# A graph-attention kernel on one core: 36 instead of 32 rows a group fetched outside GpSimd, used two groups later, and node numbers loaded earlier

## The chip, the core and the metric

The kernel runs on one core of a Trainium2 chip. The metric is the device time of one execution in microseconds (us): 2087.24 us is the median of three executions of the kernel before (2087.07 to 2089.44). One further execution was taken with the hardware profiler; its trace is where all durations below come from.

## The reference

There are N = 12500 nodes of 128 features and 212500 edges, sorted by their destination node. The layer is one block of graph attention with 8 heads of 16 features:

```
Q, K, V = x @ WQ, x @ WK, x @ WV              # N x 128 each
Eh      = edge_attr @ WE                       # one row an edge
score   = exp(clip(sum over 16 of K[src] * Q[dst] / 4 * Eh, -5, 5))    # edge x head
wV, Z   = segment sums over dst of V[src] * score and of score
h       = x + wV / (Z + 1e-6)
h       = batch norm of h over the nodes, times gamma, plus beta
out     = layer norm of (x + h) over the features
```

The irregular part is `K[src]` and `V[src]`: for each edge, one row of 256 numbers (1 KB) is fetched from a table in memory, at an address known only from the data.

## The kernel before

**Table stage.** The first 88 us project all nodes to a table `kvd` (N rows of K and V, 1 KB each) in DRAM. The inputs of the first eight groups are projected directly, so that these groups need no gather from the table.

**Groups.** The edges stand in tiles of 128 (one edge a partition). A group `g` is 8 tiles (two windows of 4), and there are 208 groups; the last has 5 tiles. One group passes through a software pipeline written out by hand: the loop `for g in range(NG - 2)` at line 820 issues, in a fixed order, pieces of groups `g - 3` to `g + 5`. Every engine runs its own instructions in that order and waits on semaphores.

- SyncE (SP) issues the loads: `load(g + 4)` for the edge features `ea` (L518, three buffers), `load_rel(g + 5)` for the relative node numbers `rb` (L429, two buffers; only for groups 0 to 15 and 204 to 207, other groups get them four at a time by `load_quad`, L415), and its share of the row fetches (below).
- GpSimd (POOL) gathers the table rows: one indirect DMA a tile (`gather`, L227), eight a group, into one of nine slots. A slot comes free when VectorE has done `message(g)` (L647), its last reader.
- VectorE (DVE) does `products(g)` (L622, which needs the gathered rows), `both_halves(g + 1)` (L601), `scores` (L629), `message(g)` (L647), the one-hot matrices (L549 to L563) and the small steps on sums.
- TensorE (PE) does the projections of edge features and queries, the turning back and the segment sums (`gather_sum`, L663).
- ScalarE (ACT) does the exponentials (`clip_exp`, L638 and L639), the copies from PSUM, the windows of the nodes (`q_window`, L538) and its share of the row fetches.

**Rows without GpSimd.** For some groups, the eighth tile isn't gathered by GpSimd. Its 128 rows are fetched by 128 plain DMAs of 1 KB each, whose addresses are read from `row_ids` into registers: one TENSOR_LOAD reads the addresses of a share (L277), then each row is one DMA (L284). `fetch_rows(g, engine, a, b)` does this in groups 8 on: 32 rows a group, the first 20 on SP's queue at the top of the iteration, the other 12 on ScalarE's queue after `q_mid(g + 3)`. Four groups fill one tile `byrow` (three buffers), and it is used three groups (`ROW_LAG`) after the group that fetched its last row: groups 14, 18, 22 and so on, 49 in all (`row_plan`). In such a group `products` works on 4, 3 and 1 tiles: the last piece waits on VectorE's queue (`rows_there`, L291) for the semaphore that counts the rows' landing.

**Node numbers.** `q_window(g)` reads two node numbers into ScalarE's registers (TENSOR_LOAD, L533) and copies two windows of 64 columns from `hx` (L538).

From group 199 on, each slot that comes free is filled by `load_x` with four blocks of x for the last stage (L505, SP's queue, after `message(g)`).

**The end.** The last two groups are written out after the loop (L874 to L935). There `share(g - 2)` (`denom`, `recip`, `attn`) stands ahead of `products(g, (0,))`; `attn` (L679) has one buffer, whose reader is `add_x` (L688) on TensorE. Then come the norms and the output, 40 us.

Of the kernel before, what the change touches and what calls it, by code (L numbers as in the profile page):

```python
# [8 lines left out]
F32 = mybir.dt.float32  # L9
BF16 = mybir.dt.bfloat16  # L10
# [7 lines left out]
P = 128  # L18
# [4 lines left out]
U = 4  # L23
# [5 lines left out]
RUN = 64  # L29
ROWS = P  # L30
FIRST_ROW = 8
ROW_LAG = 3
SP_ROWS = 20
ACT_ROWS = 12
RQ = 4
NSEM = 6

# [22 lines left out]
def row_plan(sizes):  # L60


    full = sizes.count(U) // 2
    groups, end = [], P
    while FIRST_ROW + -(-end // (SP_ROWS + ACT_ROWS)) - 1 + ROW_LAG < full:
        groups.append(FIRST_ROW + -(-end // (SP_ROWS + ACT_ROWS)) - 1 + ROW_LAG)
        end += P
    return groups
# [7 lines left out]
def gnn_kernel(  # L76
# [37 lines left out]
    wp = lps.enter_context(tc.tile_pool(name="work", bufs=2))  # L114
    tps = ExitStack()
    tab = tps.enter_context(tc.tile_pool(name="table", bufs=1))
    late = []
# [115 lines left out]
    def issue(n=0):  # L233
        while len(queued) > n:
            f, *a = queued.pop(0)
            f(*a)
# [10 lines left out]
    by_row, fill = {}, {}  # L247
    row_loads = []
    n = SP_ROWS + ACT_ROWS
    row_tiles = row_plan(usizes)  # L250
# [15 lines left out]
    def parts(g, a, b):  # L266
        return [(a, b - 1), (b - 1, b)] if g in by_row and b == G else [(a, b)]

    def fetch_rows(g, et, a, b):
        if g not in fill:  # L270
            return
        p, c, at = fill[g]
        b = min(b, tot - at)
        if b <= a:
            return
        eng = {ET.SP: nc.sync, ET.Activation: nc.scalar}[et]
        _, offs = nc.values_load_multi_w_load_instructions(  # L277
            row_ids[p:p + 1, c + a:c + b], engines=(et,), min_val=0, max_val=(N - 1) * 8 * P,
            skip_runtime_bounds_check_because="node ids")
        for r, off in enumerate(offs, at + a):  # L280
            k = row_tiles[r // P]
            if r % P == 0:
                by_row[k] = late[0].tile([P, 1, 2 * P], F32, name="byrow", bufs=3)
            d = eng.dma_start(by_row[k][r % P:r % P + 1, 0, :].bitcast(U8), kvb[ds(off, 8 * P)].unsqueeze(0))  # L284
            d.then_inc(rows_in[r // P % NSEM], 16)
            tc.no_tile_sem_insts.add(d.ins.name)
            tc.add_to_no_dep_group(f"rows{k}", d.ins)

    def rows_there(g):
        k = row_tiles.index(g)  # L290
        w = nc.vector.wait_ge(rows_in[k % NSEM], 16 * P * (k // NSEM + 1))  # L291
        tc.declare_fence(w.ins, group=f"rows{g}")

    def own(g, a, b, step):
        if g in by_row and b == G and b - a == 1:
            tc.declare_no_dep(step.ins, group=f"rows{g}", reason="the semaphore of the rows")
# [57 lines left out]
    def within(f, g):  # L354
        return f(g) if 0 <= g < NG else None
# [54 lines left out]
    RB = {}  # L410

    def load_quad(q):
        t = late[0].tile([P, RQ, U * P], BF16, name="rbq", bufs=2)
        for h in (0, 1):
            nc.sync.dma_start(t[h * WN:(h + 1) * WN].rearrange("p k d -> p (k d)"), bass.AP(  # L415
                tensor=relT[h].tensor, offset=relT[h].offset + at_half[2 * RQ * q + h] * P,
                ap=[[0, WN], [1, RQ * U * P]]))
        for k in range(RQ):
            RB[RQ * q + k] = t[:, k, :]
# [3 lines left out]
    def load_rel(g):  # L423
        if g // RQ in quads:
            return
        RB[g] = wp.tile([P, U * P], BF16, name="rb", bufs=2)
        for h in (0, 1):
            n = usizes[2 * g + h]
            nc.sync.dma_start(RB[g][h * WN:(h + 1) * WN, :n * P], bass.AP(  # L429
                tensor=relT[h].tensor, offset=relT[h].offset + at_half[2 * g + h] * P, ap=[[0, WN], [1, n * P]]))  # L430
# [76 lines left out]
    EA, OH, OT, Q3, XW, BASE, MSG, QE, OS, AT, AGG, WT, PW = ({} for _ in range(13))  # L507
# [4 lines left out]
    def halves(g):  # L512
        return [(0, usizes[2 * g]), (usizes[2 * g], nt(g))]
# [15 lines left out]
            project(g, a, lambda: turned().rearrange("p (a b) d -> p a (b d)", b=2), True)  # L529
            yield  # L530

    def q_window(g):
        _, BASE[g] = nc.values_load_multi_w_load_instructions(  # L533
            base_i[0:1, 2 * g:2 * g + 2], engines=(ET.Activation,), min_val=0, max_val=N,
            skip_runtime_bounds_check_because="node ids")
        XW[g] = wp.tile([P, P], F32, name="xw", bufs=8)
        for h in (0, 1):
            nc.scalar.activation(XW[g][:, h * WN:(h + 1) * WN], hx[:, ds(BASE[g][h], WN)], AF.Copy)  # L538
# [59 lines left out]
    def both(g, h):  # L598
        a, b = halves(g)[h]
        t = WT[g][h][:, :(b - a) * P]  # L600
        nc.vector.tensor_tensor(t, t, QE[g][h], op=OP.mult)  # L601
# [12 lines left out]
    def products(g, hs=(0, 1)):  # L614
        if 0 in hs:
            PR[g] = wp.tile([P, G, P], F32, name="p", bufs=1)
        for i in hs:
            a, b = halves(g)[i]
            for c, d in parts(g, a, b):
                if d - c == 1 and g in by_row:  # L620
                    rows_there(g)
                step = nc.vector.tensor_tensor(PR[g][:, c:d, :], KV[g](c, d, 0), PW[g][i][:, c - a:d - a, :], op=OP.mult)  # L622
                own(g, c, d, step)
# [46 lines left out]
    def denom(g):  # L670
        RZ[g] = wp.tile([P, H], F32, name="rz", bufs=2)
        nc.vector.tensor_scalar(RZ[g], OS[g][:, P:], 1e-6, None, op0=OP.add)

    def recip(g):
        nc.vector.reciprocal(RZ[g], RZ[g])

    def attn(g):
        AT[g] = wp.tile([P, P], F32, name="at", bufs=1)
        nc.vector.scalar_tensor_tensor(  # L679
            AT[g].rearrange("p (h d) -> p h d", d=DH), OS[g][:, :P].rearrange("p (h d) -> p h d", d=DH),  # L680
            keep[:, g:g + 1], RZ[g][:, :, None].to_broadcast([P, H, DH]), op0=OP.mult, op1=OP.mult)
# [46 lines left out]
    def both_halves(g):  # L728
        both(g, 0)
        both(g, 1)  # L730
# [9 lines left out]
    for q in range(NQ):  # L740
# [13 lines left out]
        k = q - first_step  # L754
# [56 lines left out]
    def within_checks(g):  # L811
        if g >= first_check and (g - first_check) % every == 0:
            check((g - first_check) // every)

    def share(g):
        denom(g)
        recip(g)
        attn(g)

    for g in range(NG - 2):  # L820
        within(load, g + 4)
        within(load_rel, g + 5)
        if (g + 6) % RQ == 0 and (g + 6) // RQ in quads:
            load_quad((g + 6) // RQ)
        fetch_rows(g, ET.SP, 0, SP_ROWS)
        within(products, g)
        within(both_halves, g + 1)
        step = within(add_x, g - 3)
        step = within(q_mm, g + 3) or step
        if step is not None and queued and g >= FIRST_ROW + 4:  # L830
            pace(step)
        issue()
        within(gather_sum, g - 1)
        if g + 1 < nxg and g + 1 not in SLOT:
            for _ in project_main(g + 1):
                pass
        within(turn_back, g + 1)
        within(scores, g)
        within(clip_exp, g)
        within(q_hi, g + 3)  # L840
        within(x_out, g - 3)
        within(sums_out, g - 1)
        within(q_lo, g + 2)
        within(denom, g - 2)
        within(recip, g - 2)
        within(attn, g - 2)
        within(q_window, g + 4)
        within(turned_onehot, g + 3)
        within(ehqe, g + 2)
        within(q_mid, g + 3)  # L850
        fetch_rows(g, ET.Activation, SP_ROWS, SP_ROWS + ACT_ROWS)
        within(message, g)
        within(onehot, g + 1)
        if g == 2:
            load_last()
        for r in runs[1:]:
            if g == max(4, r[0] // 2 - 12):
                place(r)
        within_checks(g)
        while free and todo and not pending:  # L860
            load_x()
        bn_parts(2 * g - 5, 2 * g - 3)
        if g == NG - 5:
            assert done >= set(range(NPRE))
            norm_first()
        if g == 4:
            nc.vector.tensor_scalar(row_ids, row_ids, 8 * P, None, op0=OP.mult)
        if g == FIRST_ROW - 1:
            tps.close()
            late.append(tps.enter_context(tc.tile_pool(name="late", bufs=1)))  # L870
        if g == FIRST_ROW - 2:
            free.append(NSLOT)
            load_kv()
    last = NG - 1  # L874
    g = last - 1
# [2 lines left out]
    within_checks(last)  # L878
    flag = [nc.values_load(bad_i[0:1, 0:1], min_val=0, max_val=1 << 20,
                           skip_runtime_bounds_check_because="a count")]  # L880
    share(g - 2)
    gather_sum(g - 1)
    sums_out(g - 1)
    products(g, (0,))
    both_halves(last)
    step = add_x(g - 3)
    if queued:
        pace(step)
# [313 lines left out]
```

## Time and profile before

| what | value |
|---|---|
| median of three executions | 2087.24 us (2087.07 to 2089.44) |
| the profiled execution, whole time | 2092.52 us |
| its span in the trace | 2090.7 us |
| busy: PE, DVE, POOL, ACT | 80%, 79%, 75%, 30% of the span |
| indirect DMAs from the table `kvd` | 1548, first at 88.1 us, last at 2034.4 us |
| row DMAs: SP and ACT | 3920 and 2352 (49 tiles of 128) |
| mean granted TensorE clock | 0.935 |

The profiled execution took 5.3 us more than the median; 1.8 us of it lie outside the span. In the trace's answers a line such as `DVE p L622 <- DVEq L291: 71.3, 18, 5.2` says that VectorE, ahead of line 622, waited 71.3 us in total, 18 times, at most 5.2 us, for what its own queue did at line 291. In a timeline the columns are start and length in us, engine, line, operation, output<-inputs, and in brackets the idle time ahead of it and what ended it. "SPq" and "ACTq" are instructions that a queue processor executes, DMA issues among them.

### The profile page before, as it was taken

The page shows a single profiled execution, that of the slowest core. Times are in us where ns is not written, and L with a number is a line of the kernel's source. Part 1 is how long each engine was busy: PE and PEld are TensorE (multiplying, and loading weights), DVE is VectorE, ACT ScalarE, POOL GpSimd, SP SyncE. Part 2 cuts the span into 40 slices and gives each one's busy share as a digit, 9 for nine tenths or more (in the row PEclk, how much of TensorE's full clock was granted, in tenths as well). Part 3 has the DMA queues.
Part 4 walks back from the last instruction along what each step waited for, and adds up shares of the span by engine and source line. Part 5 has one row for each costly group of instructions (what it writes and reads, how often), then busy time and mean ns, then how long its engine had stood idle before and what let it go on. Part 6 is the DMA issues. An engine that isn't in the chain of part 4 may idle for free. (4 is left out here: it accounts for less than half of the span.)

```text
span 2090.7 us, 44264 instructions
## 1 busy us (share of the span) xinstructions
PE 1676.2 (80%) x9414; PEld 1095.7 (52%) x9414; DVE 1643.1 (79%) x3679; ACT 631.2 (30%) x2480; POOL 1561.5 (75%) x1648
## 2 busy tenths in 40 slices
PE   7898888878878888878777877777787778787877
PEld 6565554555555555555455555454454445554557
DVE  4568898888888887888787877878877778887887
ACT  2343233332233332322222222322222222222226
POOL 7677777777777777777777777777777777777775
PEclk9999999999999999999999899999999999999999
DMA  8865666666666666666666666666666665665674
GB/s 288 288 190 165 181 187 183 180 181 179 189 181 188 180 180 180 188 182 182 185 172 188 171 181 177 171 180 177 172 182 176 180 179 170 180 178 171 184 238 125
DMA packets 165317, 387.29 MB, mean 185 GB/s; under 512 B 41861, under 2 KB 76846, under 8 KB 165038
## 3 DMA queue, kind: packets, MB, share of 16 engines
q0 software_dynamic: 76352, 207.20, 35.0%
q1 hardware_dynamic: 79620, 171.95, 28.1%
q10 hardware_dynamic: 9066, 5.22, 1.0%
q14 instruction: 202, 1.65, 0.3%
q8 instruction: 77, 1.26, 0.2%
HBM read 364.59 MB, written 19.63 MB: 184 GB/s over the span
## 5 line engine op out<-in xcount | busy, mean ns | idle before, releaser
L227 POOL DMA_INDIRECT slot<-kvd,srcs x1548 | 1472.3, 951 | 479.3 <-issue 410.6
L663 PE MATMUL ps_a<-msg,oh 128*128 128x136 f32 (+1 forms) x3322 | 547.6, 306 | 0.9 <-DVE msg L647 0.9
L663 PEld LDWEIGHTS ps_a<-msg,oh 128*128 128x128 f32 (+1 forms) x3322 | 443.3, 176 | 83.7 <-issue 59.2
L588 PE MATMUL ps_e<-ea,w_e 128*128 128x512 f32 x832 | 432.9, 646 | 23.2 <-DMA ea<-eaT 20.6
L622 DVE TENSOR_TENSOR p<-slot,ps_t 128x512 f32<-128x512 f32 (+1 forms) x410 | 263.7, 663 | 210.9 <-DMA slot<-kvd,srcs 192.0
L638 ACT ACTIVATE ps_m<-s 128x64 f32<-128x64 f32 (+1 forms) x209 | 47.5, 227 | 1200.5 <-DVE s L637 845.0
L609 PE MATMUL ps_t<-ident,wt 128*128 128x128 f32 x1661 | 247.3, 291 | 102.7 <-DVE wt L601 100.7
L688 PE MATMUL ps_m<-ident,at 128*128 128x128 f32 x412 | 98.1, 321 | 234.4 <-DVE oh L552 230.5
L601 DVE TENSOR_TENSOR wt<-wt,ps_q 128x512 f32<-128x512 f32 x416 | 265.2, 678 | 3.1 <-PE ps_q L596 3.1
L609 PEld LDWEIGHTS ps_t<-ident,wt 128*128 128x128 f32 x1661 | 195.9, 147 | 130.7 <-DVE wt L601 123.9
L629 DVE TENSOR_REDUCE s<-p 128x64 f32<-128x1024 f32 (+1 forms) x209 | 251.5, 1203 | 0.1
L590 ACT ACTIVATE wt<-ps_e 128x512 f32<-128x512 f32 x416 | 229.1, 585 | 44.2 <-PE ps_e L588 43.0
L647 DVE TENSOR_TENSOR msg<-slot,ps_m 128x1024 f32<-128x1024 f32 (+2 forms) x209 | 241.2, 1155 | 1.2 <-ACT ps_m L638 1.1
L688 PEld LDWEIGHTS ps_m<-ident,at 128*128 128x128 f32 x412 | 63.6, 194 | 325.3 <-ACT q L578 308.3
L588 PEld LDWEIGHTS ps_e<-ea,w_e 128*128 128x128 f32 x832 | 156.4, 209 | 142.8 <-issue 93.6
L596 PE MATMUL ps_q<-ot,q 64*128 64x512 bf16 x1248 | 173.1, 384 | 0.0
L596 PEld LDWEIGHTS <-q 64*128 64x128 bf16 x1248 | 44.5, 95 | 194.9 <-issue 170.1
L549 DVE TENSOR_TENSOR oh<-ps_m,rel_i 128x512 f32<-128x512 f32 x208 | 141.6, 681 | 0.0
L538 ACT ACTIVATE xw<-hx 128x64 f32 x416 | 84.0, 248 | 102.2 <-issue 86.6
L679 DVE SCALAR_TENSOR_TENSOR at<-os,keep,rz 128x128 f32<-128x128 f32 x208 | 73.1, 352 | 25.8 <-PE ps_m L688 1.5
L693 ACT ACTIVATE hx<-ps_m 128x64 f32 x412 | 90.7, 220 | 8.1 <-PE ps_m L689 1.2
L569 PE MATMUL ps_m<-w_q,xw 128*128 128x128 f32 x416 | 85.7, 290 | 3.2 <-DVE oh L552 2.7
(174 smaller groups left out, 1568.6 us busy)
## 6 DMA issues: line engine op xcount, KB each, us to landing
ea<-eaT SPq DMA_DIRECT2D x207, 512.0 KB
byrow<-kvd SPq DMA_DIRECT2D x3920, 1.0 KB
byrow<-kvd ACTq DMA_DIRECT2D x2352, 1.0 KB
slot<-kvd,srcs POOLq DMA_INDIRECT x1548
rbq<-relT SPq DMA_DIRECT2D x94, 256.0 KB
kvd<-slot SPq DMA_DIRECT2D x12, 512.0 KB
kvd<-t SPq DMA_DIRECT2D x12, 512.0 KB
slot<-xT SPq DMA_DIRECT2D x24, 256.0 KB
```

What stands on the lines that cost most here:

```text
L227: return nc.gpsimd.indirect_dma_start(out=out, out_offset=None, in_=table, in_offset=bass.IndirectOffsetOnAxis(ap=srcs[:, e:e + 1], axis=0))
L549: nc.vector.tensor_tensor(one, iota_ps[:, None, :].to_broadcast([P, n, P]), r[:, :n, None].to_broadcast([P, n, P]), op=OP.is_equal)
L588: nc.tensor.matmul(eh, w_e, EA[g][:, a:b, :].rearrange("p a b -> p (a b)"), start=True, stop=True)
L590: nc.scalar.activation(t[:, :(b - a) * P], eh, AF.Copy)
L596: nc.tensor.matmul(QE[g][h], Q3[g][r, k, :], OT[g][r, :(b - a) * P], start=(k == 0), stop=(k == 2))
L601: nc.vector.tensor_tensor(t, t, QE[g][h], op=OP.mult)
L609: nc.tensor.transpose(ps[:, j, :], WT[g][h][:, j * P:(j + 1) * P], ident)
L622: step = nc.vector.tensor_tensor(PR[g][:, c:d, :], KV[g](c, d, 0), PW[g][i][:, c - a:d - a, :], op=OP.mult)
L629: nc.vector.tensor_reduce(SS[g][:, a:b, :], PR[g][:, a:b, :].rearrange("p t (h d) -> p t h d", d=DH), axis=AX.X, op=OP.add)
L647: step = nc.vector.tensor_tensor(MSG[g][:, a:b, :P].rearrange("p t (h d) -> p t h d", d=DH), KV[g](a, b, P).rearrange("p t (h d) -> p t h ...
L663: nc.tensor.matmul(AGG[g][WN if j >= n else 0:], OH[g][j], MSG[g][:, j, :], start=(j == 0), stop=(j == n - 1))
L688: nc.tensor.matmul(ps, AT[g], ident, start=True, stop=False)
```

## The change

- `SP_ROWS` 20 to 21 and `ACT_ROWS` 12 to 15: 36 rows a group, so that a tile is filled in 3.6 groups.
- `ROW_LAG` 3 to 2 and `byrow` with two buffers: a tile is used two groups after its last fetch. With both, the groups that use one are 13, 17, 20, 24, 27, 31 and so on to 205: 55 tiles. The last fetch, in group 203, holds 20 rows, all of them SP's.
- `rb` has three buffers.
- The reading of the node numbers becomes `q_base`, which the loop calls for group `g + 4` ahead of `scores` and `clip_exp`; on ScalarE's queue the TENSOR_LOAD then stands after the row fetches of the iteration before and ahead of the exponentials.
- At the end, `attn(g - 2)` comes after `products(g, (0,))` and `both_halves(last)`; `gather_sum(g - 1)` and `sums_out(g - 1)` are written after it. TensorE's order stays as it was.

```
-ROW_LAG = 3
-SP_ROWS = 20
-ACT_ROWS = 12
+ROW_LAG = 2
+SP_ROWS = 21
+ACT_ROWS = 15
...
-                by_row[k] = late[0].tile([P, 1, 2 * P], F32, name="byrow", bufs=3)
+                by_row[k] = late[0].tile([P, 1, 2 * P], F32, name="byrow", bufs=2)
...
-        RB[g] = wp.tile([P, U * P], BF16, name="rb", bufs=2)
+        RB[g] = wp.tile([P, U * P], BF16, name="rb", bufs=3)
...
-    def q_window(g):
+    def q_base(g):
         _, BASE[g] = nc.values_load_multi_w_load_instructions(
             base_i[0:1, 2 * g:2 * g + 2], engines=(ET.Activation,), min_val=0, max_val=N,
             skip_runtime_bounds_check_because="node ids")
+
+    def q_window(g):
+        if g not in BASE:
+            q_base(g)
...
         within(turn_back, g + 1)
+        within(q_base, g + 4)
         within(scores, g)
...
-    share(g - 2)
-    gather_sum(g - 1)
-    sums_out(g - 1)
+    denom(g - 2)
+    recip(g - 2)
     products(g, (0,))
     both_halves(last)
+    attn(g - 2)
+    gather_sum(g - 1)
+    sums_out(g - 1)
     step = add_x(g - 3)
```

More of the change, by code (lines that the diff above doesn't have):

```diff
@@ L880, in gnn_kernel @@
                            skip_runtime_bounds_check_because="a count")]
-    share(g - 2)
+    denom(g - 2)
+    recip(g - 2)
+    products(g, (0,))
+    both_halves(last)
+    attn(g - 2)
     gather_sum(g - 1)
     sums_out(g - 1)
-    products(g, (0,))
-    both_halves(last)
     step = add_x(g - 3)
```

## The prediction

> **What bounds the kernel now.** I read the page's groups first, then the waits of each engine, then the timeline of SP and VectorE, then the end. GpSimd comes first:
>
> ```profile
> L227 POOL DMA_INDIRECT slot<-kvd,srcs x1548 | 1472.3, 951 | 479.3 <-issue 410.6
> ```
>
> ```profile
> POOL slot L227 <- issue: 426.5, 1397, 0.3
> ...
> POOL slot L227 <- DVE msg L647: 3.7, 4, 2.8
> ```
>
> One gather is 0.95 us, and 0.30 us of issue stand ahead of nearly every one; GpSimd has waited for a free slot for 3.7 us only. The first starts at 88.1, the last at 2034.4: 1946.3 us for 1547 steps, 1.258 us each, with no hole. So the length between table and end is the number of gathers times 1.258. With 32 rows a group from elsewhere a group costs GpSimd (8 - 32/128) x 1.258 = 9.75 us.
>
> VectorE runs freely at 7.5 us a group (first products at 188.53, 196.04, 203.56) and waits for two things, one after the other in the run. From 200 to 880 us:
>
> ```profile
> DVE p L622 <- DVEq L291: 71.3, 18, 5.2
> ...
> DVE p L622 <- DMA slot<-kvd,srcs: 4.1, 5, 1.8
> ```
>
> and from 900 to 2030 us:
>
> ```profile
> DVE p L622 <- DMA slot<-kvd,srcs: 183.2, 89, 5.1
> ```
>
> Up to 880 us the row tile is late, later the gathers are. The late row is SP's, which issues without a pause:
>
> ```profile
> 361.58 0.37 SPq L518 DMA_DIRECT2D ea<-eaT  x1
> 363.53 6.38 SPq L284 DMA_DIRECT2D byrow<-kvd  x20
> 370.01 0.37 SPq L518 DMA_DIRECT2D ea<-eaT  x1
> 371.96 6.43 SPq L284 DMA_DIRECT2D byrow<-kvd  x20
> 378.49 0.37 SPq L518 DMA_DIRECT2D ea<-eaT  x1
> 378.91 1.10 SPq L415 DMA_DIRECT2D rbq<-relT  x2
> ```
>
> The hole of 1.5 us ahead of each train of rows is the TENSOR_LOAD of its addresses (1.44). Group 10's first row starts at 202.83, group 106's at 1062.27: 8.95 us a group, hardly a wait in it. VectorE uses a row 5 to 8 us after SP's last issue (group 30: last issue over at 361.47, use at 366.82). SP is thus slower than VectorE, faster than GpSimd, and it started late:
>
> ```profile
> 170.73 1.08 SPq L429 DMA_DIRECT2D rb<-relT  x2
> 171.85 0.58 SPq L518 DMA_DIRECT2D ea<-eaT  x1
> 178.32 1.08 SPq L429 DMA_DIRECT2D rb<-relT  x2
> 181.24 6.45 SPq L284 DMA_DIRECT2D byrow<-kvd  x20
> ```
>
> From 172.5 to 178.3 SP waited with `rb` of group 13 for the buffer that `turned_onehot(11)` (L559) was still reading.
>
> **The change part by part.**
>
> *Gathers.* 55 row tiles instead of 49: 1542 gathers, 6 x 1.258 = 7.5 us less on the chain that sets the end. This is the gain.
>
> *SP, 21 rows.* One more row: a step is 0.332 us (mean from row to row between 200 and 1050 us). One more address: the TENSOR_LOAD takes 0.48 for 2 addresses, 0.77 for 12, 1.37 for 20 (shortest of each); between the first two 0.03 an address, between the last two 0.075. I take 0.03 and keep 0 and 0.075. That makes 8.95 + 0.36 = 9.31 us a group (9.28 to 9.36). GpSimd will need (8 - 36/128) x 1.258 = 9.71. SP stays the faster, by 0.4 us.
>
> *Lag 2, and `rb` with three buffers.* A row is wanted one group sooner, some 8 us, while SP is already late. Against it SP starts sooner: `rb` of group 13 then waits for `turned_onehot(10)` (over at 170.7), and what ends last is the `ea` load, which needs the projection of group 9 (over at 171.6). So ea at 171.7, rb at 172.3, addresses at 173.5 instead of 179.5: 6 us. VectorE's position is set back by 8 - 6 - (rounding of the tile's end) in the first groups. Is GpSimd then blocked on slots? Group g needs the slot of group g - 9. Groups 17 and 18 have it at once or 2.6 us early, as now; group 22 starts its gathers at 228.9 and `message(13)` ended at 218.3. The wait for the first tile, at group 13, will be about 6 us, so some 3 us of margin remain after the one gather less. GpSimd isn't blocked: 0, at worst 3 us (start not advanced).
>
> *Two `byrow` buffers.* The first row of tile k + 2 is issued at least three groups after the last of tile k, 2 x 9.31 us and more of SP's time; tile k is used some 6 us after its last row and read a last time 6 us later. 12 against 18: no wait.
>
> *ScalarE.* Three more rows, 0.345 each by its mean step: 1.0 us. From the exponential at 1015.96 to the last row issued at 1022.75 are 6.8 us; with the rows, the address read ahead (0.67) and its gap, less the 0.43 that `xw` waited for it, 8.1 us a group. That is more than VectorE's 7.5, less than SP's 9.31; it takes slack, 0 on the end. The last row's landing, 6.3 + 4.7 + 4 us after a group's second products, comes before the use two groups on at 15.8; barely, and it would be swallowed by the wait for SP or GpSimd. In groups 3 to 7, where ScalarE's evacuations come right ahead of the exponentials, the read delays them by at most 0.1 each: 0.4 us, bounds 0 and 2. The added load of `row_ids` and the wider memset: 0.3, bounds 0 and 0.5.
>
> *VectorE.* A group with a row tile takes 0.2 us longer; 6 more, 1.2 us spread over the run, hidden under its waits. If the cover were gone: 1.2.
>
> *The end.* Here VectorE waits at
>
> ```profile
> 2032.78 0.35 DVE L679 SCALAR_TENSOR_TENSOR at<-os,keep,rz 128x128 f32<-128x128 f32 x1 [1.47 <-PE ps_m L688]
> 2033.05 0.68 DVE L622 TENSOR_TENSOR p<-slot,ps_t 128x512 f32<-128x512 f32 x1
> 2033.64 0.88 DVE L601 TENSOR_TENSOR wt<-wt,ps_q 128x384 f32<-128x384 f32 x2
> 2034.44 0.55 DVE L622 TENSOR_TENSOR p<-slot,ps_t 128x384 f32<-128x384 f32 x1
> ```
>
> with the products of group 206 behind it. Moved, products and both halves run from 2031.3, `attn` at 2032.8, the second products at 2033.05: 1.4 us less. VectorE's last stretch without a hole begins with the second products of group 205 at 2024.07. That group becomes a row group, so its last gather ends 7.5 + 1.26 us sooner and its row would be wanted at 2024.07 + 0.55 - 8.8 = 2015.8. SP's chain says when it's there. Group 8's first row at 181.2 - 6 = 175.2, group 10 at 21.6 later, group 199 after 189 x 8.95 = 1692 and 191 x 0.36 = 69: 1957.4. From there to group 203 it was 50.15 (four blocks of x each time, L505), 1.6 of it a wait for `rb`'s buffer that goes: 48.6 + 4 x 0.36 = 50.0, so 2007.4. Its 20th row is issued 6.2 later, 2013.6, and lands 3.4 (as at the end now) to 8 us on: 4.5, 2018.1. So VectorE waits 2.3 us there; its next operation starts at 2018.3 instead of 2024.67: -6.4, with `attn` -7.8. It can't come sooner than the last gather: 2035.3 - 7.5 + 3.8 = 2031.6 for the last products, now at 2041.03, -9.4.
>
> *Sum.* -7.8 + 0.4 + 0.3 = -7.1, -7 taken: 2085.5 against the profiled 2092.5, and 2080.2 against the median of 2087.24, since the 5.3 us between them are not the change's.
>
> **The rivals.**
>
> *SP is a little dearer and becomes the bound (slower).* It has to issue 196 groups in a row; each 0.01 us a group is 2 us at the end. Up to 0.35 there is no wait at group 205 at all and -9 stands; at 0.36, -7; at 0.39 the gain is gone; at 0.42, through fetches of code or a dearer address, it is +4.7. For it: SP is at work all the time, and the blocks of x at the end hit it. Against it: the row step of 0.332 hardly varies. 0.16, of which 0.05 fall within 0.2%.
>
> *SP is cheaper.* -9, the bound set by the last gather. 0.13.
>
> *The start isn't advanced* (another wait holds SP's first row, such as the row tiles' place, which the table's buffers must leave; their last reader ends at 172.1, against). Then the whole of SP's chain is 6 us later, and GpSimd stops 3 us at group 22: -1 to +3. 0.08.
>
> *The transfers bound it, whoever issues them.* The DMA engines are 62 to 66% busy all along (by stretches of 330 to 560 us), and the gathers' chain is made of 0.95 + 0.30 us on GpSimd, not of landings; the bytes are the same. Then: 0, less the 1.4 of the end. 0.04. The Trainium skill has this as a rule against the change: on the page "DMA: Bandwidth & Descriptors", section "Issuing engines are not separate DMA queues", all queues run on the same 16 engines, and issuing from several saves only the time to initiate a DMA, usually small. By that rule the sum would be about -1; here the time to initiate is 1.258 us of GpSimd's chain for each tile, so the trace doesn't bear it out.
>
> **How the numbers follow.** Forecast 0.59, all faster; cheaper SP 0.13, faster; dearer SP 0.16 (0.05 same, 0.11 slower); late start 0.08 (0.06 same, 0.02 slower); transfers 0.04 (same). Changes within 0.2%, 4.2 us, are what a measurement of this kernel can hardly tell from none. Faster 0.72, same 0.15, slower 0.13. The range leaves out about 2 in 10: from -10.2 (the bound at -9 and 1.2 of the runs' spread) to +0.8 over the two cases near none, 2077 to 2088.
>
> **What would show it.** Right: 1542 gathers back to back at 1.258, the last near 2027; SP's first row near 175; 9.3 us from train to train; VectorE's waits at L291 grown to 150 to 250 us in some 40 of 55 tiles and those for gathers shrunk below 100, with the length set by neither. `attn` without a wait. Wrong: a hole of GpSimd at groups 17 to 30; a train step of 9.4 or more; a wait of over 5 us at L291 in group 205.

## The result, and the profile after

The changed kernel takes 2392.41 us (median of four, 2390.69 to 2394.97) against 2087.59 us for the kernel before (2087.07 to 2089.44): a ratio of 1.146, 95% interval 1.144 to 1.148. The forecast was 2080.2. The time went up by 305 us.

In the runs called disturbed below, the kernel before took 3092 to 3164 us (medians) as well, and in the traces SP's trains of 20 or 21 rows took 11.0 to 12.5 us (medians) instead of 6.4 to 6.8, from a cause that isn't known; from those runs only the lengths of single address loads are used.

The page of the changed kernel names the engine at once. These are its chain of work that ended last (by engine, then by line) and three of its groups. Lines from L538 on stand four to seven lower than before: L642 is the exponential, L697 `x_out`, L581 `qr` of `q_mid`, L563 `turned_onehot`, L533 now the reading in `q_base`.

```profile
ACTq 40%; issue 27%; ACT 16%; PE 10%; DVE 5%; DMA 2%; POOL 0%; DVEq 0%; SPq 0%
ACTq L284 30%; ACTq L533 6%; ACT wt L594 4%; ACTq L277 3%; PE ps_a L667 3%; ACT xw L542 3%; ACT hx L697 2%; ACT ps_m L642 2%; ACT q L582 1%; DVE msg L651 1%; ACT os L672 1%; PE ps_e L592 1%; PE ps_t L348 1%; ACT q L577 1%; PE ps_t L613 1%
...
L227 POOL DMA_INDIRECT slot<-kvd,srcs x1542 | 1459.7, 947 | 728.0 <-issue 385.2
...
L581 DVE SCALAR_TENSOR_TENSOR qr<-ps_m,q 128x128 f32<-128x128 f32 x208 | 60.6, 291 | 616.3 <-ACT hx L697 611.7
L642 ACT ACTIVATE ps_m<-s 128x64 f32<-128x64 f32 (+1 forms) x209 | 47.5, 227 | 1664.6 <-PE ps_e L592 670.8
```

ScalarE's queue and ScalarE hold 56% of the chain, the row fetches (L284) alone 30%, though ScalarE computes for only 600 us. The exponential's idle 1664.6 us is the time in which its own queue reads addresses and issues rows. The releasers printed ahead of it are mostly matmuls that don't feed it. In the lap below the one printed ends at 1042.12, while VectorE's scores have been ready since 1039.17 and the queue's read of the node numbers ends last, at 1042.68. The waits of all engines, then SP's, show who stands behind it:

```profile
DVE qr L581 <- ACT hx L697: 611.7, 199, 5.1
PE ps_m L692 <- DVE oh L556: 542.9, 192, 5.2
...
POOL slot L227 <- PE ps_m L573: 295.0, 177, 4.3
```

```profile
SPq L518 <- PE ps_e L592: 335.8, 133, 11.2
```

In 199 groups VectorE waits 3 us, by the profile for the copies to `hx`; `message`, the one-hot matrices and the products stand behind that wait. TensorE waits for the one-hots, GpSimd's first gather of a group for the `q_mm` that paces it, and SP's `ea` load, with the rows behind it, for the projection that frees its buffer. There is no wait at L291 in the whole run. One lap of ScalarE, in its timeline (start and length in us; ACTq is its queue):

```profile
1031.85 0.23 ACT L642 ACTIVATE ps_m<-s 128x64 f32<-128x64 f32 x1 [8.59 <-PE ps_q L600]
1032.01 0.24 ACT L643 ACTIVATE msg<-s 128x64 f32<-128x64 f32 x1
1032.15 0.26 ACT L577 ACTIVATE q<-ps_m 128x128 bf16<-128x128 f32 x1
1032.31 0.47 ACT L697 ACTIVATE hx<-ps_m 128x64 f32 x2
1032.68 0.28 ACT L672 ACTIVATE os<-ps_a 128x136 f32<-128x136 f32 x1
1032.84 0.40 ACT L542 ACTIVATE xw<-hx 128x64 f32 x2
1033.13 1.08 ACT L594 ACTIVATE wt<-ps_e 128x512 f32<-128x512 f32 x2
1034.09 0.33 ACT L582 ACTIVATE q<-qr 128x128 bf16<-128x128 f32 x1
1036.73 5.15 ACTq L284 DMA_DIRECT2D byrow<-kvd  x15
1042.83 0.23 ACT L642 ACTIVATE ps_m<-s 128x64 f32<-128x64 f32 x1 [8.41 <-PE ps_t L613]
```

and the same place before:

```profile
1018.76 0.31 ACT L578 ACTIVATE q<-qr 128x128 bf16<-128x128 f32 x1
1018.82 3.93 ACTq L284 DMA_DIRECT2D byrow<-kvd  x12
1024.30 0.23 ACT L638 ACTIVATE ps_m<-s 128x64 f32<-128x64 f32 x1 [5.23 <-DVE s L637]
```

Before, the first row follows `q_mid` at once, and after the last row ScalarE waits 1.5 us for VectorE's scores. After, there are 2.3 us between `q_mid` and the first row, and the lap closes on itself: 10.98 us from exponential to exponential, with no wait for another engine in it. So the granted TensorE clock, 0.871 after and 0.935 before, isn't what makes the lap long. The 2.3 us are not shown as work; they are the end of the TENSOR_LOAD of the row addresses (L277), which the view of the tile `row_ids` gives as shortest/median/longest in ns. Before:

```profile
L277 SPq TENSOR_LOAD <-row_ids x196: 1372/1442/1764, 179.5 to 2014.0; - x196
L277 ACTq TENSOR_LOAD <-row_ids x196: 768/810/992, 179.5 to 2009.5; - x196
```

and after:

```profile
L277 SPq TENSOR_LOAD <-row_ids x196: 1383/1662/1954, 171.9 to 2313.1; - x196
L277 ACTq TENSOR_LOAD <-row_ids x195: 3226/3377/3571, 178.0 to 2304.8; - x195
```

Three more addresses, 15 for 12, and ScalarE's load takes 3.38 us instead of 0.81. It starts while ScalarE still computes, so 2.3 of it stand in the lap. GpSimd's gathers, unbroken before, have a hole in nearly every group:

```profile
1034.35 0.95 POOL L227 DMA_INDIRECT slot<-kvd,srcs  x1 [0.30 <-issue]
1037.46 0.94 POOL L227 DMA_INDIRECT slot<-kvd,srcs  x1 [2.17 <-PE ps_m L573]
1038.71 0.95 POOL L227 DMA_INDIRECT slot<-kvd,srcs  x1 [0.30 <-issue]
```

The last gather starts at 2269.9 us, not at 2027, and the exponential of group 207 comes 75 us behind it.

### The profile page after: what moved, and what is told of

It reads as the page before. It is cut to its first block, busy times and chain, and to the rows that moved or that the text cites. A ratio compares the mean times of both kernels' runs of the same rounds, so it can differ in the third digit from the quotient of the medians.

```text
span 2393.2 us, 45857 instructions
## 1 busy us (share of the span) xinstructions
PE 1773.3 (74%) x9414; PEld 1228.0 (51%) x9414; DVE 1653.0 (69%) x3691; ACT 600.2 (25%) x2480; POOL 1548.5 (65%) x1642
## 4 chain that ended last, share of the span: by engine, by line
ACTq 40%; issue 27%; ACT 16%; PE 10%; DVE 5%; DMA 2%; POOL 0%; DVEq 0%; SPq 0%
ACTq L284 30%; ACTq L533 6%; ACT wt L594 4%; ACTq L277 3%; PE ps_a L667 3%; ACT xw L542 3%; ACT hx L697 2%; ACT ps_m L642 2%; ACT q L582 1%; DVE msg L651 1%; ACT os L672 1%; PE ps_e L592 1%; PE ps_t L348 1%; ACT q L577 1%; PE ps_t L613 1%
## 5 line engine op out<-in xcount | busy, mean ns | idle before, releaser
L667 PE MATMUL ps_a<-msg,oh 128*128 128x136 f32 (+1 forms) x3322 | 669.9, 354 | 0.8 <-DVE msg L651 0.8
L667 PEld LDWEIGHTS ps_a<-msg,oh 128*128 128x128 f32 (+1 forms) x3322 | 557.7, 215 | 99.9 <-issue 87.8
L692 PE MATMUL ps_m<-ident,at 128*128 128x128 f32 x412 | 121.0, 385 | 552.6 <-DVE oh L556 542.9
L581 DVE SCALAR_TENSOR_TENSOR qr<-ps_m,q 128x128 f32<-128x128 f32 x208 | 60.6, 291 | 616.3 <-ACT hx L697 611.7
L642 ACT ACTIVATE ps_m<-s 128x64 f32<-128x64 f32 (+1 forms) x209 | 47.5, 227 | 1664.6 <-PE ps_e L592 670.8
L592 PE MATMUL ps_e<-ea,w_e 128*128 128x512 f32 x832 | 391.1, 592 | 0.7 <-ACT wt L594 0.7
L651 DVE TENSOR_TENSOR msg<-slot,ps_m 128x1024 f32<-128x1024 f32 (+3 forms) x209 | 240.7, 1153 | 0.4 <-ACT ps_m L642 0.3
L613 PE MATMUL ps_t<-ident,wt 128*128 128x128 f32 x1661 | 217.3, 273 | 2.1 <-ACT t L325 0.6
L573 PE MATMUL ps_m<-w_q,xw 128*128 128x128 f32 x416 | 109.4, 357 | 3.1 <-DVE oh L556 2.7
L693 PE MATMUL ps_m<-xw,ident 128*128 128x128 f32 x412 | 105.9, 350 | 0.0
L573 PEld LDWEIGHTS ps_m<-w_q,xw 128*128 128x128 f32 x416 | 90.2, 267 | 5.1 <-issue 2.5
```

Of the source, the lines that this page charges most:

```text
L592: nc.tensor.matmul(eh, w_e, EA[g][:, a:b, :].rearrange("p a b -> p (a b)"), start=True, stop=True)
L613: nc.tensor.transpose(ps[:, j, :], WT[g][h][:, j * P:(j + 1) * P], ident)
L651: step = nc.vector.tensor_tensor(MSG[g][:, a:b, :P].rearrange("p t (h d) -> p t h d", d=DH), KV[g](a, b, P).rearrange("p t (h d) -> p t h ...
L667: nc.tensor.matmul(AGG[g][WN if j >= n else 0:], OH[g][j], MSG[g][:, j, :], start=(j == 0), stop=(j == n - 1))
L692: nc.tensor.matmul(ps, AT[g], ident, start=True, stop=False)
```

## The experiments

The theories. **A (the start):** the load is dear because the addresses now start at column 21 of their row of `row_ids`, no multiple of four. **B (the number):** more than 12 addresses, or an odd number, are dear. **C (the place):** the node numbers read ahead make ScalarE's loads dear. Later **D**: something else of the change costs too, **E**: ScalarE's lap counts in full, **F**: the shorter lag.

### What makes the load dear

The kernel before with other shapes of read, the same rows being fetched:

```
+        k = g % 8
...
-            row_ids[p:p + 1, c + a:c + b], ...
+            row_ids[p:p + 1, c + a - (k if a else 0):c + b + (0 if a else k)], ...
...
+        offs = offs[k:] if a else offs[:b]
```

> The kernel before, with reads of other shapes and the same rows fetched: in group g, with k = g mod 8, ScalarE reads its addresses from column 20 - k on (12 + k addresses, the last 12 used), and SP reads 20 + k from column 0 (the first 20 used). Theory A (the start): ScalarE's loads are cheap from columns 20 and 16 (0.8 and 1.0 us) and dear from 13, 14, 15, 17, 18 and 19: 0.22 for each address, 2.9 to 4.2 us. SP's grow by 0.22 for each address past a multiple of four. Theory B (the number): all with more than 12 are dear, the 16 from column 16 too. Theory C (the place): none is dear, under 1.3 us all. The time of the whole: by A a group on ScalarE is 6.8 + 2 on the mean = 8.8 to 9.3, under GpSimd's 9.75, so 2087 to 2150 us.

Measured, median of about 25 loads of each shape:

| ScalarE: first column | 20 | 19 | 18 | 17 | 16 | 15 | 14 | 13 |
|---|---|---|---|---|---|---|---|---|
| addresses | 12 | 13 | 14 | 15 | 16 | 17 | 18 | 19 |
| us | 0.82 | 2.94 | 3.14 | 3.37 | 1.07 | 3.82 | 4.03 | 4.25 |

From columns 20 and 16 the load is cheap, from the six others it costs 0.22 us for each address (a straight line through the six points has that slope and 0.07 us at nought). 16 addresses from column 16 are cheaper than 13 from 19. All eight of ScalarE's reads end at column 32, so the number of addresses is a multiple of four exactly where the start is: the table alone doesn't tell the two apart. SP's reads do. They all start at column 0, and with odd numbers took 1.67 us (21), 2.06 (23), 1.90 (25) and 2.30 (27), where 0.22 an address would be 4.6 to 5.9. So a number that is no multiple of four is not dear from such a start; what is left beyond a multiple of four costs some 0.2 each, over 1.44 for 20 in the kernel before. (SP's loads of even numbers scatter in this disturbed run, those of 24 between 0.11 and 1.76, and are left out.) A holds, B falls; on ScalarE itself no such number was read from such a start. The kernels that followed agree. The changed kernel with one column more read:

```
-            row_ids[p:p + 1, c + a:c + b], ...
+            row_ids[p:p + 1, c + a // 4 * 4:c + b], ...
...
+        offs = offs[a % 4:]
```

> The changed kernel, but ScalarE's read of its row addresses (L277) starts one column earlier, at column 20 instead of 21 of its row of row_ids, and the first of the 16 addresses is dropped. Theory A (the start): the load took 3.4 us instead of 0.8 because it starts at a column that is no multiple of four, so that each of the 15 addresses costs 0.22 us by itself. From column 20 it takes 0.9 to 1.1 us, a group on ScalarE falls from 10.98 to 8.6 us, GpSimd's gathers run back to back again, and the time is what the prediction gave, 2075 to 2090 us. Theory B (the number): more than 12 addresses, or an odd number, are dear on ScalarE: the load of 16 takes 3.4 us or more and the time stays at 2390 or above. Theory C (the place): the node numbers read ahead of the exponentials make ScalarE's loads dear, whatever the start: 3.4 us, 2390.

the changed kernel without `within(q_base, g + 4)`:

> The changed kernel without the node numbers read ahead: they are read in q_window, as in the kernel before. Theory A (the start) and theory B (the number): the load of 15 addresses still takes 3.4 us. 0.78 and a gap of 0.15 leave the line ahead of the exponentials, about 0.45 come back ahead of the copies of the windows: 10.5 us a group instead of 10.98, 195 x 0.48 = 94 us less, about 2300 us (2280 to 2320). Theory C (the place): the load takes 0.9 us again, and the time is 2075 to 2090.

and with `SP_ROWS` 20 and `ACT_ROWS` 16:

> The changed kernel with the 36 rows a group shared as 20 by SP and 16 by ScalarE, whose addresses then start at column 20. Theory A (the start): the load takes 0.9 to 1.1 us, a group on ScalarE 8.6 + 0.35 = 8.9 to 9.0 us, one on SP 8.95; both under GpSimd's 9.71: 2072 to 2090 us. Theory B (the number): 3.5 us and more, a group over 11.2 us, above 2430 us. Theory C (the place): the load stays at 3.4 us, above 2390 us.

ScalarE's load took 1.05, 3.37 and 1.05 us: C falls too. All four runs were disturbed, so their times tell nothing; undisturbed ones follow further down, but not for the second kernel.

The Trainium skill says on its page "Runtime: NRT & Kernel Launch", section "Instruction fetch mechanics", that a TENSOR_LOAD costs about 200 ns a register, in bulk as well; it says so of the registers that the runtime loads, while the row here is a tile of the kernel. The six dear shapes agree with that (0.22 us); 12 addresses in 0.82 and 16 in 1.07 us do not, and here the measurement decides.

### What the load costs the kernel

The first of these kernels again, undisturbed:

> The changed kernel with ScalarE's addresses read from column 20 (16 of them, the first dropped), for a time that is not disturbed: in the two runs so far every engine's queue stopped for some 10 us in most groups, in the kernel before just as here. Theory A (the load of 15 addresses from column 21 is the whole loss): 8.7 us a group on ScalarE, gathers at 1.258, 2075 to 2090 us against 2087 for the kernel before. Theory D (something else of the change costs too): above 2110 us.

2133.68 us (2131.04 to 2136.76), ratio 1.022 (1.020 to 1.024). The one column takes away 259 of the 305 us, but the kernel is still slower than before, so D holds: A explains 85% of the loss and not all of it. Tile `row_ids` and the waits of this run (lines one lower again):

```profile
L277 SPq TENSOR_LOAD <-row_ids x196: 1392/1688/2021, 172.1 to 2056.0; - x196
L277 ACTq TENSOR_LOAD <-row_ids x195: 1010/1057/1234, 178.2 to 2038.1; - x195
```

```profile
DVE qr L582 <- ACT hx L698: 247.6, 173, 5.1
...
DVE p L627 <- DVEq L292: 93.3, 23, 11.1
```

The gathers are nearly unbroken again: 1.261 us each on the mean, the last at 2029.8. But VectorE is far behind them: its last products start at 2080.3, 50 us after the last gather, where before they started 7 us after. VectorE waits for ScalarE's copies in 173 groups. SP too has become slower than forecast: 9.59 us a group from group 8 to 104, 8.99 before. It waits no more than before: from its last row to the next address load are 0.85 us on the mean, 0.84 before. Its last address load starts at 2056.0, 42 us later than the 2014.0 of before, and VectorE's last long wait of the run is for the rows that follow it, in group 205 (SP's queue, then VectorE):

```profile
2057.54 6.44 SPq L285 DMA_DIRECT2D byrow<-kvd  x20
```

```profile
2058.27 1.14 DVE L627 TENSOR_TENSOR p<-slot,ps_t 128x512 f32<-128x512 f32 x2
2065.33 0.29 DVE L627 TENSOR_TENSOR p<-byrow,ps_t 128x128 f32<-128x128 f32 x1 [5.91 <-DVEq L292]
```

This is the third sign that the prediction named for a wrong forecast. With the load repaired, SP's chain ends the run.

### Where the other 46 us are

20 and 16 rows, which gives both queues cheap loads:

```
-SP_ROWS = 21
-ACT_ROWS = 15
+SP_ROWS = 20
+ACT_ROWS = 16
```

> The changed kernel with 20 rows by SP and 16 by ScalarE (addresses from columns 0 and 20), for an undisturbed time. The run with 21 and 15 and a cheap read on ScalarE left SP at 9.59 us a group where the prediction had 9.31: its load of 21 addresses took 1.69 us, that of 20 takes 1.44. Theory A, for both queues (an address beyond a multiple of four costs 0.2 us on either): SP is back at 8.95 to 9.0 us a group, ScalarE at 8.5 + 0.35 = 8.9, GpSimd's 9.71 sets the length again, and the gain of the prediction comes: 2077 to 2082 us against 2087.6. Theory E (ScalarE's longer group, which VectorE waits for in each group, costs by itself): 2088 us or more.

2142.84 us (2138.96 to 2153.31), ratio 1.025 (1.023 to 1.027). The gain that A promised for two cheap loads doesn't come: SP's load is back at 1.43 us and the time has not dropped. But the row that SP gave up went to ScalarE, so this doesn't say that SP was not what held the run before. VectorE's waits and SP's:

```profile
DVE qr L581 <- ACT hx L697: 342.2, 187, 5.1
```

```profile
SPq L518 <- PE ps_e L592: 215.9, 87, 11.2
```

SP has time to wait (1.54 us from last row to next load); here ScalarE's lap holds it. The same without the node numbers read ahead:

```
-        within(q_base, g + 4)
```

> 20 rows by SP, 16 by ScalarE, both loads cheap, and the node numbers read in q_window as in the kernel before. With the read ahead this gave 2142.8 us (ratio 1.0249): SP's load of 21 addresses, theory A's second half, was not what held it, ScalarE's group took 9.73 us on the mean (8.7 where it waits for nothing, and 1.0 of waits for TensorE and VectorE on the mean), every group of it in VectorE's way. Theory E (ScalarE's group counts in full): taking the read from the head of the exponentials takes 0.95 us from the line and gives 0.57 back ahead of the windows, so 9.35 us a group and 2143 - 190 x 0.38 = 2071, bounded below by the gathers at 2078: 2076 to 2095 us. If the read ahead has no part in it (the rows themselves hold VectorE up): 2130 us or more.

2117.00 us (2108.85 to 2123.54), ratio 1.014 (1.012 to 1.017). The read ahead costs about one hundredth of the time, some 22 us of 2087, with these shares; both E's 2076 to 2095 and the 2130 or more of the other case are missed. The rows alone, in the kernel before:

```
-ACT_ROWS = 12
+ACT_ROWS = 16
```

> The kernel before with one part of the change: 36 rows a group, 20 by SP and 16 by ScalarE (both loads cheap), still used three groups later from three buffers, rb with two, the node numbers and the end as before. With the lag of two, three rb buffers and the new end the same share gave 2117.0 us (ratio 1.0144), VectorE waiting 186 us for ScalarE's copies to hx, 93 us for rows and 31 us for gathers. Theory E (ScalarE's group of 8.8 us, waits for TensorE in it, is too long whatever the lag): VectorE's wait for hx stays near 186 us and the time near 2117 us (2105 to 2125). Theory F (the shorter lag: rows are waited for, the wait delays ScalarE's next rows, and so on): the wait for rows falls under 40 us and the time to 2080 to 2095 us.

2113.23 us (2106.94 to 2119.51), ratio 1.013 (1.011 to 1.015): no different from the run with the shorter lag, within the intervals. F's 2080 to 2095 is missed, though VectorE's waits for rows, 68.8 us, did not fall under the 40 that it named either; the four rows alone cost 26 us. The timeline of ScalarE and the waits of VectorE:

```profile
1338.10 0.30 ACT L578 ACTIVATE q<-qr 128x128 bf16<-128x128 f32 x1
1338.97 5.37 ACTq L284 DMA_DIRECT2D byrow<-kvd  x16
1344.45 0.23 ACT L638 ACTIVATE ps_m<-s 128x64 f32<-128x64 f32 x1 [6.04 <-PE ps_e L588]
```

```profile
DVE qr L577 <- ACT hx L693: 223.7, 158, 5.0
...
DVE p L622 <- DVEq L291: 68.8, 25, 5.5
```

The exponential starts 0.1 us after the last row: ScalarE no longer waits for the scores, VectorE waits for ScalarE. But SP, with its 20 rows a group as before, is slower here as well: 25 of its 196 trains (groups 31, 35, 39 and so on) take 7.8 to 9.6 us instead of 6.5, 54 us in all, and it steps at 9.40 us from group 8 to 104 with no more waiting than before. VectorE's last long waits in the loop are for `rb`, which SP's queue loads:

```profile
2018.72 0.35 DVE L559 TENSOR_SCALAR ot<-rb,wiota 128x512 bf16<-128x512 bf16 x1 [3.23 <-DMA rb<-relT]
2033.60 0.35 DVE L559 TENSOR_SCALAR ot<-rb,wiota 128x512 bf16<-128x512 bf16 x1 [7.22 <-DMA rb<-relT]
```

Why these trains are slow is open; the run with the shorter lag has 3 trains of that kind. So the 26 us are not ScalarE's alone, and F isn't cleanly ruled out. Counted over 184 groups in the middle of each run:

| kernel | ScalarE's lap without its wait ahead of the exponential, us | exponential right behind the last row, or behind the node numbers read after it | exponentials, group 8 to the last: us a step, of 200 | ratio |
|---|---|---|---|---|
| before | 7.45 | 30 of 184 | 9.33 | 1 |
| before, 20 and 16 | 9.14 | 159 | 9.44 | 1.013 |
| after, 20 and 16, read in place | 8.87 | 144 | 9.42 | 1.014 |
| after, cheap load | 9.07 | 158 | 9.53 | 1.022 |
| after, 20 and 16 | 9.53 | 166 | 9.64 | 1.025 |
| after | 10.84 | 173 | 10.85 | 1.146 |

The last two columns rise together nearly by themselves, since 200 such steps are nine tenths of the run (the kernels at 9.42 and 9.44 lie within each other's intervals). The weight is on the other two: in every slower kernel the exponential follows ScalarE's queue in most groups. In "after" and "after, 20 and 16" the lap all but fills the step, and SP waits. In "after, cheap load" and "before, 20 and 16" the lap leaves 0.5 and 0.3 us of the step, and SP's own step, without more waits than before, is as long (9.59 and 9.40 from group 8 to 104); these runs don't separate the two queues. With the read in place neither fills the step, and what holds that kernel is open.

One thing else is in the 26 us of "before, 20 and 16". VectorE waits once in each of these runs but that of the changed kernel, near group 107, for a row of numbers (`thr`, L477) that SP's queue loads behind its rows: 2.9 us before, 6.1 to 14.2 in the three changed kernels with a cheap load, and 19.1 here. A kernel whose gathers set the length may make that up; one whose lap sets it can't. So of these 26 us up to 16 may be that single wait. No run takes it away, and how the 26 split is open.

### Two that told nothing

The kernel before with its own 12 addresses read as 13 from column 19:

> The kernel before, with ScalarE's 12 addresses read as 13 from column 19, one column earlier than before: 2.94 us instead of 0.82, nothing else changed, 32 rows a group. ScalarE's group, with its waits for TensorE, takes 7.5 us of the 9.38 in the kernel before; with this 9.6. The kernels with ScalarE's group at 9.73 and 9.48 us on the mean took 2143 and 2113 to 2117. Theory E (ScalarE's group counts in full as soon as it is over some 9.3 us, the time from first to last exponential of the kernel before over 200 groups): 2115 to 2150 us. If only the new parts of the change cost, and ScalarE has slack up to GpSimd's 9.75: 2087 to 2095 us.

The load took 2.93 us. All three runs of this kernel were disturbed (ratio 0.98 each time, from which nothing follows). The other two, with what was expected of them:

> The kernel before, with ScalarE's addresses read from column 19 instead of 20 (13 of them, the first dropped); everything else is as before. The load takes 2.94 us instead of 0.82, as the table of starts showed. Theory A with the slack that the prediction counted: ScalarE's group is 6.8 + 2.1 = 8.9 us, still under SP's 8.95 and GpSimd's 9.75, so the time hardly moves: 2087 to 2100 us. If ScalarE's slack is smaller than that (the exponentials are waited for by VectorE and TensorE in every group), above 2120 us.

> The kernel before with ScalarE's 12 addresses read as 13 from column 19, at 2.94 us instead of 0.82. If ScalarE has the slack that the prediction counted (6.8 us of work a group, 8.9 with this), the time hardly moves, as SP needs 8.99 and GpSimd 9.75: 2087 to 2100 us. If the load is in a loop with VectorE and TensorE that has less slack: above 2120 us.

What the dear load alone does to the kernel before stays open.

A version made from the findings: 34 rows, 20 and 14, the rows of `row_ids` 36 columns apart, 16 addresses read from column 20, node numbers read in place, the rest as in the change:

```
-SP_ROWS = 21
-ACT_ROWS = 15
+SP_ROWS = 20
+ACT_ROWS = 14
...
-        fill[FIRST_ROW + q] = (q % P, q // P * n, q * n)
+        fill[FIRST_ROW + q] = (q % P, q // P * 36, q * n)
...
-            row_ids[p:p + 1, c + a:c + b], ...
+            row_ids[p:p + 1, c + a:c + (b + 3) // 4 * 4], ...
...
+        offs = offs[:b - a]
...
-        within(q_base, g + 4)
```

> A version made from what the runs showed: 34 rows a group, 20 by SP and 14 by ScalarE, both reads at whole multiples of four columns (the rows of row_ids stand 36 columns apart, ScalarE reads 16 from column 20), two groups later in two buffers, rb with three, the new end, and the node numbers read in place. 52 tiles, so three gathers fewer than before (3.8 us). ScalarE's group is 0.7 us shorter than with 16 rows, 8.1 us and its waits. Theory E: that leaves ScalarE under 9.3 us on the mean, and the kernel gains the gathers and the end's 1.4 us: 2080 to 2087 us. If ScalarE's group still counts: 2090 to 2105 us.

This run was disturbed too: ratio 0.999 (0.997 to 1.001) with the kernel before at 3096 us. Whether it gains is open, and no kernel here beat the one before in an undisturbed run.

### Further disturbed runs

These are further runs of kernels shown above, with what was expected of them. Their load lengths repeat those given, their times tell nothing.

The changed kernel reading from column 20 (ScalarE's load 1.05 us):

> The changed kernel with ScalarE's addresses read from column 20 (16 of them, the first dropped). In the first run the load took 1.05 us instead of 3.37, but every queue of that chip issued slowly, so that its time tells nothing. Theory A (the load is the whole loss): a group on ScalarE is 10.98 - 2.3 = 8.7 us, GpSimd's gathers stand at 1.258 again, 2075 to 2090 us. Theory D (something else of the change costs too: the node numbers ahead of the exponentials, or the shorter lag): the time comes back only in part and stays above 2110 us, with GpSimd still waiting for its pace.

20 and 16 rows (1.05 us), twice:

> The changed kernel with 20 rows by SP and 16 by ScalarE, whose addresses start at column 20 (the load took 1.05 us in the first run, on a chip whose queues were slow). Theory A: 8.7 + 0.35 = 9.0 us a group on ScalarE, 8.95 on SP, both under GpSimd's 9.71; SP's last row comes earlier than with 21, so 2074 to 2088 us. Theory D: above 2110 us.

> The changed kernel with 20 rows by SP and 16 by ScalarE (addresses from columns 0 and 20). The run with 21 and 15 and a cheap read on ScalarE left SP at 9.59 us a group (groups 8 to 104) where the prediction had 9.31: its load of 21 addresses took 1.69 us, that of 20 took 1.44. Theory A, now for both queues (an address beyond a multiple of four costs 0.2 us on either): SP is back at 8.95 to 9.0 us a group, ScalarE at 8.5 + 0.35 = 8.9, GpSimd's 9.71 sets the length again, and the gain of the prediction comes: 2087.6 less 7 to 10, 2077 to 2082 us. Theory E (ScalarE's longer group, which VectorE waits for in each group, costs by itself): 2088 us or more.

The changed kernel with the node numbers read in place (3.37 us), twice; the 2300 us expected of it was never put to the test:

> The changed kernel without the node numbers read ahead; the load of 15 addresses from column 21 took 3.37 us in the first run, as in the changed kernel. Theory A: 10.98 - 0.93 + 0.45 = 10.5 us a group, about 2300 us (2280 to 2320). Theory D with the node numbers as its cause: below 2200 us.

> The changed kernel (21 and 15, ScalarE's load from column 21 at 3.37 us) without the node numbers read ahead. Theory A: ScalarE's order is the loop, so 0.93 leave it and about 0.45 come back: 10.5 us a group, 2300 us (2280 to 2320). If the read ahead is a cause of its own: below 2200 us.

20 and 16 rows, node numbers read in place (1.05 us):

> The kernel with 20 and 16 rows, without the node numbers read ahead. Theory A: both orders keep ScalarE below SP and GpSimd, so the time is that of the one with the read ahead within 3 us. Theory E (ScalarE's group is what counts): some 0.45 us a group less on ScalarE, and a time lower by 10 us or more.

## Why the prediction was wrong, step by step

*ScalarE* is the step that failed first: "8.1 us a group ... it takes slack, 0 on the end". It cost 259 of the 305 us through one load. Three things in it were wrong.

First, the load of 15 addresses was costed at nothing. The working priced an added address on SP (0.03, bounds 0 and 0.075) and none on ScalarE, though the same edit moved ScalarE's first address from column 20 to 21. The load grew by 2.57 us, and the 2.3 of it that stand in the lap are most of the way from 8.1 to 10.98. The price of an address came from loads of 2 and 12 numbers on ScalarE and 20 on SP. No row of the profile before showed a read of `row_ids` that starts off a multiple of four; only the two node numbers are read from such columns in every other group, and there the start makes no difference (0.67 us either way). That is where a bound from both sides was owed. The figure of the Trainium skill ("Runtime: NRT & Kernel Launch", "Instruction fetch mechanics") could have been such a bound, though the 12 addresses in 0.81 us spoke against it: 15 registers at 200 ns are an estimate of 3.0 us. By that estimate the lap is 8.1 + 2.2 = 10.3, over SP's 9.31 by 1.0 us in each of 196 groups, and the forecast a loss of some 190 us.

Second, the slack. The 6.8 us were read off one quick lap; the mean lap, with its waits for TensorE and slower trains of rows, is 7.45. And all below SP's 9.31 was taken to be free. The exponentials of the kernel before follow each other at 9.33, as the gathers, at 9.75 a group, start at 88 us and have a lead; but laps of 9.14 and 8.87 us, both under that, came with 26 and 27 us lost, in which SP had a part.

Third, "takes slack" overlooked who stands behind ScalarE. VectorE's `q_mid` waits for ScalarE's copies in 199 groups, `message` and everything for the next lap stand behind `q_mid`, and ScalarE's rows come after its own part of `q_mid`. A queue so long is not hidden: in the changed kernel it is the loop. The read ahead, costed at 0.4 us in a few early groups, cost some 22 us with 20 and 16 rows.

*SP*: the row step held (0.332 us after as before), the added address did not: 1.66 us for 21 against 1.44 for 20, so 0.22 where 0.075 was the upper bound. With the row that is 0.55 us a group, and 0.60 was measured with the cheap load on ScalarE (9.59 against 8.99). The rival "SP is a little dearer" had this mechanism and went only to 0.42. By its own scale, 2 us for each 0.01 over 0.39, 0.60 gives +42. This is the second step that failed: with the load on ScalarE repaired the kernel is 46 us slower, SP waits no more than before, and VectorE's last long wait, 5.91 us in group 205, is for its rows. That both numbers come so near is in part luck, since ScalarE's lap was nearly as long, and VectorE waited 247.6 us for ScalarE's copies against 93.3 for rows.

*Start and buffers* held. SP's first row stands at 173.9 us, for 175.2 forecast:

```profile
170.70 1.09 SPq L429 DMA_DIRECT2D rb<-relT  x2
173.91 6.80 SPq L284 DMA_DIRECT2D byrow<-kvd  x21
```

No fetch waited for a `byrow` buffer, and with the cheap load GpSimd's waits for a slot's last reader sum to 5.6 us.

*Gathers*: 1542, and with the cheap load nearly back to back, the last at 2029.8 for "near 2027". The step was right and worth nothing, for the end was no longer theirs. VectorE's waits for rows, forecast at 150 to 250 us in some 40 tiles, were 93.3 in 23 there and none in the changed kernel.

*The end*: `attn` lost its wait, as forecast, in the kernel with the cheap load (VectorE's timeline):

```profile
2072.07 0.69 DVE L627 TENSOR_TENSOR p<-slot,ps_t 128x512 f32<-128x512 f32 x1
2072.68 0.88 DVE L606 TENSOR_TENSOR wt<-wt,ps_q 128x384 f32<-128x384 f32 x2
2073.57 0.35 DVE L684 SCALAR_TENSOR_TENSOR at<-os,keep,rz 128x128 f32<-128x128 f32 x1
2073.83 0.68 DVE L627 TENSOR_TENSOR p<-slot,ps_t 128x512 f32<-128x512 f32 x1
```

In the changed kernel it still waits 1.17 us for TensorE. Its 1.4 us are too small to be told apart.

*The rivals*: none had ScalarE as the bound. The signs named for a wrong forecast were all on GpSimd and SP. Two showed in the changed kernel, holes of GpSimd in groups 17 to 30 and SP's trains at 10.9 us instead of 9.31, and both were effects there; the third, the wait in group 205, showed with the cheap load. The transfers did not bind: the DMA engines are about 55% busy after.

## What to carry to other kernels

An engine that also issues DMAs, as ScalarE here, has one queue for both, so its lap must be added up as a whole, address loads included and on the mean rather than from a quick lap, and held against the pace of the whole kernel whenever another engine waits for it in each lap. When an edit changes how many things a queue reads, look also at where the read starts: a shape that the trace of before doesn't contain has no price yet. A wait that is put down to a matmul which doesn't feed the instruction, in front of an engine whose queue issues rows, is a reason to look at that queue in the timeline. And once one bound is repaired, the next queue has to be priced again: here SP stood close behind ScalarE.

## What the runs showed of the hardware

- Loading row addresses from a row of 4-byte numbers into an engine's registers: 12 in 0.82 us and 16 in 1.07 us if the first stands at a multiple of four columns, 0.22 us for each address otherwise (13 in 2.94, 19 in 4.25; all on ScalarE). Starts two columns off (14 addresses in 3.14, 18 in 4.03) are as dear as odd ones. A read of two numbers takes 0.67 us from either kind of start.
- From a start at a multiple of four, each address beyond a multiple of four costs some 0.2 us (on SP 20 in 1.44 and 21 in 1.66 us, 25 in 1.90 and 27 in 2.30).
- The share of busy time hides this altogether: ScalarE was busy for 25% of the span when its queue set the pace of everything.
